# Reordering the attention slots that carry a cycle of the twist network

## The chip, the cores and the metric

The kernel runs as one program on one core of a Trainium2 chip. Its time is the device time in microseconds (us). The core's engines run side by side, each through its own list of instructions in order: TensorE (PE in the profile, PEld for its weight loads), VectorE (DVE), ScalarE (ACT), GpSimd (POOL) and SyncE (SP), which here only issues DMAs. An instruction waits on semaphores that other engines raise, and everything behind it on its own engine waits with it. TensorE writes its results to PSUM, which has eight banks of 128x512 float32.

## The reference, cut to what matters

The model has two layers over `x` of shape (32, 128, 128). The change touches the first layer alone, where an attention is followed by a mixing network:

```python
x = x + attn0(cond(x))             # 16 heads of 64, causal, softmax, output projection
h = recurrence(x)                  # sigmoid gates, two running products, a running sum
gf = global_net(h.mean(axis=1))    # once for each sequence
for _ in range(3):                 # the three cycles of the twist network
    tf = sigmoid(gelu(gelu(gelu(out @ w1) @ w2) @ w3) @ w4)   # 128 -> 128 -> 64 -> 32 -> 1
    coupling = 0.1 + range * (0.7 * gf + 0.3 * tf - 0.5) * 2
    out = out + coupling * twist(out)      # twist: a signed permutation of the 128 features
x = x + out
```

The second layer (routed experts, an attention with small heads, a low-rank layer, slots) follows. It is not touched.

## The kernel before, in words

Everything is float32, with features on the 128 partitions. The 4096 tokens stand as eight chunks of 512 columns, and a chunk is four sequences of 128.

**The slots of the first attention.** The loop `for h in range(NH)` goes over 16 half-chunks (a chunk, and half of its heads), and inside it `for b in range(CB)` goes over four sequences. One pass of the inner loop is called a slot here and is named by h and b: h10 b2. There are 64 of them. A slot pushes one unit of attention, `unit(h, b)` (L462), into a hand-made pipeline, `Staggered(0, 3, 4, 5)` (L825). So a slot does the `scores` of its own unit, then `turned` of the unit three slots older, `values` of the unit four slots older, and, in every fourth slot, `projected` of the unit five slots older.

- `scores` (L474): on TensorE two causal-mask matmuls in bf16 (`causal`, `twice`) that open two PSUM banks, and 32 records of small `qk` matmuls. On VectorE, for each bank, the row maximum (`s_max<-ps`), a tiny minimum (`s_max<-s_max`) and the biased copy `s_sb<-ps,s_max`. On ScalarE four exponentials out of the two banks and one in place. On GpSimd `s_half` and `s_part`, which halve the rows for the sums. On VectorE `s_sum` and its reciprocal. On GpSimd the normalising `s_sb<-s_sb,s_sum`.
- `turned` (L519): six transposes (`ps<-w_base,s_sb`), copied out by ScalarE (`pT`, 512 columns) and VectorE (`pT`, 256 columns).
- `values` (L531): 32 small matmuls (`ps<-pT,v` and `ps<-pT,vo`), copied out by VectorE (`oT`).
- `projected` (L544): four matmuls of 128x512.

Beside the units, a slot takes one step of every running generator (`recurrence`, L556, and `routed`, L680) and three of the twelve `projections` of the next half-chunk: one matmul of 128x512 each, copied out by ScalarE as `qk` or `v`.

**The slots with a cycle.** In seven slots (h6, h7, h8, h10, h11, h12 and h14, always at b2) a cycle of `twisted` (L594) runs for two chunks at once, in steps. A cycle is numbered 0, 1 or 2: h6, h10 and h14 have cycle 0; h7 and h11 cycle 1; h8 and h12 cycle 2.

- `first`: two matmuls of 128x512 (`ps<-F,w_mix`) and two gelus (`h`). `second`, `third`: two smaller matmuls and one gelu each. Cycle 0 adds three tiny matmuls of the global network with activations `g`, `g` and `tg`.
- `fourth` (L648): two matmuls, two tanh (`th<-ps,hb`), and then the coupling. For each chunk: VectorE `th<-th,ar,cB`; GpSimd `v<-th,F` (not in cycle 2); VectorE `th<-th,TF`; VectorE or GpSimd `F<-F,th`; VectorE or GpSimd `tw<-TF,v`; in cycle 2 GpSimd `X<-X,F`. `TF` is the twisted F. In cycle 0 it comes from a matmul with `twist` and stays in a PSUM bank until `tw` has been read out of it; in the other cycles it is in SBUF.

The slot alternates these steps with its three projections: first, projection, second, projection, third, projection, fourth. At h14 `prepared` (L755), some thirty small matmuls for the second layer, runs in the same slot.

**What sets the order.** A scheduler orders each engine's instructions, with two exceptions. Every activation that goes through `act` (L381) keeps the program's order on ScalarE. VectorE and TensorE instructions that are issued while the list `pinned` is not empty keep the program's order among themselves. PSUM banks are handed out by `ps()` (L297) in a ring of eight, `RING = "AABBBCCC"`: a ninth request waits until a bank of the same letter has been read out. Nearly all instructions are recorded at two helper lines, L259 (TensorE, VectorE, GpSimd) and L383 (ScalarE), so they are told apart by their tiles.

Of the kernel before, what the change touches and what calls it, by code (L numbers as in the profile page):

```python
# [11 lines left out]
F32 = mybir.dt.float32  # L12
# [7 lines left out]
P = 128  # L20
# [5 lines left out]
CH = CB * S  # L26
# [192 lines left out]
class Staggered:  # L219
# [7 lines left out]
        self.items.append(stages)  # L227
        self._step()

    def _step(self):  # L230
        for k, lag in enumerate(self.lags):
            n = self.t - lag
            if 0 <= n < len(self.items) and k < len(self.items[n]) and self.items[n][k]:
                self.items[n][k]()
        self.t += 1

    def flush(self):
# [7 lines left out]
def program(ctx, tc, out, xT, packs, where):  # L245
    nc = tc.nc
    pinned = []
# [35 lines left out]
    def w(name):  # L283
        pack, rows, c0, n = where[name]
        return loaded[pack][:rows, c0 : c0 + n]
# [8 lines left out]
    def bank(tag):  # L294
        return psum.tile([P, 512], F32, tag="ps" + tag, name="ps", bufs=RING.count(tag))

    def ps():  # L297
        if short:
            return bank("C")
        turn["all"] += 1  # L300
        return bank(RING[(turn["all"] - 1) % 8])
# [5 lines left out]
    def mm(out_, lhsT, rhs, start=True, stop=True):  # L307
        T.matmul(out_, lhsT=lhsT, rhs=rhs, start=start, stop=stop)

    def inner(ap, n):  # L310

        return ap.unsqueeze(2).to_broadcast([ap.shape[0], ap.shape[1], n])
# [5 lines left out]
    def tt(eng, out_, a, b, op):  # L318
        eng.tensor_tensor(out_, a, b, op)
# [7 lines left out]
    def col(g):  # L327
        return X[:, bass.ts(g, CH)]

    def b3(ap):  # L330

        return ap.rearrange("p (b s) -> p b s", s=S)
# [48 lines left out]
    def act(*args, **kwargs):  # L381

        return tc.keep_in_program_order(A.activation(*args, **kwargs))  # L383
# [7 lines left out]
    tpool = ctx.enter_context(tc.tile_pool(name="t2", bufs=2, side="right"))  # L391
# [34 lines left out]
    def modulated(g):  # L426
        bs = slice(g * CB, (g + 1) * CB)
        xs = qpool.tile([P, CH], F32, tag="xs", name="xs", bufs=1)
        tt(G, b3(xs), b3(col(g)), inner(ysT[:, bs], S), ALU.mult)
        p = ps()  # L430
        mm(p, w("cond_w"), xs)
        hTs[g] = qpool.tile([P, CH], F32, tag="hT", name="hT")
        tt(V, b3(hTs[g]), b3(p), inner(dT[:, bs], S), ALU.mult)
# [120 lines left out]
    Fs = {}  # L554
# [39 lines left out]
    def twisted(g0, cyc, turned):  # L594

        gs = (g0, g0 + 1)
        bs = slice(g0 * CB, (g0 + 2) * CB)
        nb = 2 * CB
        at = {}

        def first():
            at["h1"] = []
            for g in gs:
                p = ps()
                mm(p, w("cn_w1"), Fs[g])
                h1 = mpool.tile([P, CH], F32, tag="h1", name="h1")
                act(h1, p, AF.Gelu, bias=w("cn_b1"))
                at["h1"].append(h1)
            if cyc == 0:
                gct = mpool.tile([P, nb], F32, tag="gct", name="gct")  # L610
                for k, g in enumerate(gs):
                    V.tensor_reduce(gct[:, k * CB : (k + 1) * CB], b3(Fs[g]), AX.X, ALU.add)
                V.tensor_scalar(gct, gct, 1.0 / S, None, ALU.mult)
                p = ps()
                mm(p[:64, :nb], w("gc_w1"), gct)
                at["g1"] = mpool.tile([64, nb], F32, tag="g1", name="g1")
                act(at["g1"], p[:64, :nb], AF.Gelu, bias=w("gc_b1"))

        def second():

            p = ps()
            for k in range(2):
                mm(p[64 * k : 64 * k + 64], w("cn_w2"), at["h1"][k])
            at["h2"] = mpool.tile([P, CH], F32, tag="h2", name="h2", bufs=1)
            act(at["h2"], p, AF.Gelu, bias=w("cn_b2"))
            if cyc == 0:
                p = ps()
                mm(p[:32, :nb], w("gc_w2"), at["g1"])
                at["g2"] = mpool.tile([32, nb], F32, tag="g2", name="g2")
                act(at["g2"], p[:32, :nb], AF.Gelu, bias=w("gc_b2"))  # L630

        def third():
            p = ps()
            for k in range(2):
                r = slice(64 * k, 64 * k + 64)
                mm(p[32 * k : 32 * k + 32], w("cn_w3")[r], at["h2"][r])
            at["h3"] = mpool.tile([64, CH], F32, tag="h3", name="h3", bufs=1)
            act(at["h3"], p[:64], AF.Gelu, bias=w("cn_b3"))
            if cyc == 0:

                p = ps()
                mm(p[:, :nb], w("gc_w3"), at["g2"])
                tg = mpool.tile([P, nb], F32, tag="tg", name="tg")
                act(tg, p[:, :nb], AF.Tanh, bias=hb3, scale=0.5)
                cBs[g0] = mpool.tile([P, nb], F32, tag="cB", name="cB")
                V.tensor_scalar(cBs[g0], tg, ar7, 0.1, ALU.mult, ALU.add)

        def fourth():  # L648
            two = [ps(), ps()]
            for k in range(2):  # L650
                r = slice(32 * k, 32 * k + 32)
                mm(two[k], w("cn_w4")[r], at["h3"][r])
            for k, g in enumerate(gs):
                th = mpool.tile([P, CH], F32, tag="th", name="th")
                act(th, two[k], AF.Tanh, bias=hb4, scale=0.5)
                cB = cBs[g0][:, k * CB : (k + 1) * CB]
                V.scalar_tensor_tensor(b3(th), b3(th), ar3, inner(cB, S), ALU.mult, ALU.add)

                F, TF = Fs[g], turned[k]
                if cyc == 0:  # L660
                    p = ps()
                    mm(p, w("twist"), F)
                    TF = p
                if cyc < 2:
                    v = mpool.tile([P, CH], F32, tag="h1", name="v")
                    tt(G, v, th, F, ALU.mult)
                tt(V, th, th, TF, ALU.mult)
                tt(G if k else V, F, F, th, ALU.add)
                if cyc < 2:
                    tt(V if cyc == 0 else G, turned[k], TF, v, ALU.subtract)  # L670
                if cyc == 2:
                    tt(G, col(g), col(g), Fs[g], ALU.add)

        return [first, second, third, fourth]


    picks = {}
# [143 lines left out]
    NH = 2 * NCH  # L821
# [3 lines left out]
    pipe = Staggered(0, 3, 4, 5)  # L825
    turned = {}
    running = []
    for h in range(NH):


        pieces = projections(h + 1) if h + 1 < NH else []
        for b in range(CB):
            pipe.push(*unit(h, b))
            for gen in list(running):
                if next(gen, gen) is gen:
                    running.remove(gen)
            if b == 1 and h >= 3 and h % 2 == 1:
                gen = recurrence((h - 3) // 2, [apool.tile([P, CH], F32, tag="rec%d" % i, name="rec", bufs=1) for i in range(3)])
                next(gen)
                running.append(gen)  # L840
            if b == 0 and h % 2 == 0 and h + 2 < NH:
                modulated(h // 2 + 1)
            work = []
            k = h - 6
            if h == NH - 1 and b == 2:
                pinned_g.append(True)
            if b == 2 and 0 <= k < NH - 7 and k % 4 < 3:
                if k % 4 == 0:
                    turned = [tpool.tile([P, CH], F32, tag="t2", name="tw") for _ in range(2)]
                work = twisted(2 * (k // 4), k % 4, turned)  # L850
                if h == NH - 2:
                    prepared()
            if b == 3 and k >= 0 and k % 4 == 2:
                running.append(routed(2 * (k // 4)))
            for i in range(4):
                if work:
                    work[i]()
                if i < 3 and pieces:
                    pieces[3 * b + i]()

# [523 lines left out]
    def first_pieces():  # L1386
# [16 lines left out]
        def cycle(g0, cyc, turned, k, n):  # L1403

            several(*ins[k : k + n])
            for i, f in enumerate(twisted(g0, cyc, turned)):
                several(f, *outs[k + i : min(k + i + 1, k + n)])
# [117 lines left out]
    for i in range(END + 2 * TURN):  # L1525
        r, k = i // TURN, i % TURN
# [6 lines left out]
        if r < NP and k == 0:  # L1533
            ins, outs, _ = (p + q for p, q in zip(experts(2 * r), experts(2 * r + 1)))
# [3 lines left out]
        if k >= 24 and r < NP:  # L1538
            b = k - 23
# [49 lines left out]
```

## Time and profile before

| | us |
|---|---|
| median of 3 runs | 1243.85 |
| lowest to highest | 1240.15 to 1244.99 |
| the profiled execution, its own time | 1245.78 |
| its span on the core | 1244.0 |
| TensorE busy | 1093.5 (88%) |
| VectorE busy | 753.7 (61%) |
| ScalarE busy | 694.8 (56%) |
| GpSimd busy | 446.6 (36%) |
| slots of the first attention, first scores to last | 35.6 to 581.5 |

The profile is one execution. Some 2 us lie around its span, and it stands 1.9 us above the median. A group's row gives its busy time, the mean duration in ns of one instruction, and the idle time of the engine ahead of the group with what ended most of it. A row of the timeline gives start, length, engine, operation, tiles and count, and in brackets the idle time of the engine ahead of it and who ended it. A float32 matmul of 128x512 stands in the trace as two records. The granted clock of TensorE is a share of its full speed.

### The profile page before, as it was taken

The numbers are of one execution on the slowest core, as the hardware profiler recorded it, in microseconds if no ns is written. First come the engines' busy times: TensorE is split into PE (matmuls) and PEld (weight loads), VectorE is DVE, ScalarE is ACT, GpSimd is POOL, SyncE is SP. The second block draws the span as 40 slices with busy tenths as digits, with TensorE's granted clock in tenths as the row PEclk, the third lists the DMA queues.
The fourth block names the chain that finished last, engine by engine and source line by source line (L and its number), as shares of the span: only waits on it lengthen the run. The fifth ranks groups of instructions, "written<-read, shape, count | busy, mean of one in ns | idle before, by whom it ended". The sixth has DMA issues, their size and how long they took to land. (4 is left out here: it accounts for less than half of the span.)

```text
span 1244.0 us, 28751 instructions
## 1 busy us (share of the span) xinstructions
PE 1093.5 (88%) x11429; PEld 693.2 (56%) x11429; DVE 753.7 (61%) x2254; ACT 694.8 (56%) x1668; POOL 446.6 (36%) x557
## 2 busy tenths in 40 slices
PE   3999999988999889998888677998999999998774
PEld 1465555445454454554545445776676676676543
DVE  1454858475595755937446478456746674757654
ACT  1655464554646646445455556665875586558631
POOL 1445545435454454523354531133212321222000
PEclk9999999899999999989998898999999999999867
DMA  6000000000000000000242210234023502320000
GB/s 268 18 10 11 9 10 11 9 4 8 9 10 10 3 8 9 10 3 8 97 134 66 85 40 3 70 113 135 11 78 95 162 12 62 110 67 11 2 17 17
DMA packets 23460, 56.46 MB, mean 45 GB/s; under 512 B 2592, under 2 KB 12960, under 8 KB 23072
## 3 DMA queue, kind: packets, MB, share of 16 engines
q0 software_dynamic: 9648, 40.01, 10.3%
q1 hardware_dynamic: 13104, 13.58, 3.7%
q8 instruction: 90, 1.47, 0.5%
q10 hardware_dynamic: 576, 1.05, 0.3%
q14 instruction: 42, 0.34, 0.1%
HBM read 46.25 MB, written 2.10 MB: 39 GB/s over the span
## 5 line engine op out<-in xcount | busy, mean ns | idle before, releaser
L383 ACT ACTIVATE s_sb<-ps,s_max 128x128 f32<-128x128 f32 x256 | 73.8, 366 | 125.3 <-DVE s_sb L259 120.1
L259 PE MATMUL ps<-hT,w_attn 128*128 128x512 f32 x256 | 127.0, 624 | 15.5 <-DVE hT L259 10.1
L259 POOL TENSOR_TENSOR s_sb<-s_sb,s_sum 128x512 f32<-128x512 f32 (+1 forms) x126 | 106.8, 868 | 66.6 <-DVE s_sum L259 59.6
L383 ACT ACT_TABLE_LOAD x63 | 80.8, 1283 | 80.3 <-DVE s_sb L259 66.6
L259 POOL DMA_INDIRECT ew<-in_expert,rows x64 | 63.4, 991 | 130.3 <-DVE ye L259 79.3
L383 ACT ACTIVATE qk<-ps 128x512 f32<-128x512 f32 x128 | 72.5, 607 | 60.6 <-PE ps L259 59.8
L259 DVE TENSOR_REDUCE s_max<-ps 128x6 f32<-128x384 f32 x128 | 64.4, 541 | 50.9 <-PE ps L259 50.8
L259 POOL TENSOR_TENSOR s_half<-s_sb 128x256 f32<-128x256 f32 x62 | 45.8, 739 | 134.1 <-ACT s_sb L383 134.1
L383 ACT ACTIVATE he<-ps,ew 128x128 f32<-128x128 f32 x256 | 71.7, 384 | 32.1 <-issue 18.7
L259 PEld LDWEIGHTS ps<-hT,w_attn 128*128 128x128 f32 x256 | 47.4, 196 | 74.2 <-issue 44.0
L259 PE MATMUL ps<-pT,v 128*64 128x64 f32 (+1 forms) x1536 | 83.8, 229 | 3.5 <-DVE X L259 1.9
L383 ACT ACTIVATE s<-ps,s1max 128x128 f32<-128x128 f32 x256 | 73.1, 390 | 18.9 <-DVE s1max L259 18.9
L259 PEld LDWEIGHTS ps<-pT,v 128*64 128x64 f32 (+1 forms) x1536 | 70.6, 138 | 21.8 <-issue 5.0
L259 PE MATMUL ps<-he,ew 128*128 128x128 f32 x512 | 77.0, 291 | 5.9 <-ACT he L383 4.9
L259 PEld LDWEIGHTS ps<-he,ew 128*128 128x128 f32 x512 | 67.8, 197 | 25.2 <-ACT he L383 12.9
L259 PE MATMUL ps<-X,ew 128*128 128x128 f32 x512 | 76.8, 282 | 0.9 <-DMA ew<-in_expert,rows 0.9
L259 PEld LDWEIGHTS <-twice 128*128 128x128 bf16 x384 | 36.1, 98 | 71.9 <-issue 61.4
L259 DVE TENSOR_REDUCE s1m<-ps 128x6 f32<-128x384 f32 x128 | 65.0, 548 | 16.3 <-PE ps L259 16.3
L259 DVE TENSOR_REDUCE s_sum<-s_part 128x8 f32<-128x256 f32 x62 | 25.8, 415 | 80.6 <-POOL s_part L259 80.5
L259 PEld LDWEIGHTS ps<-X,ew 128*128 128x128 f32 x512 | 67.0, 193 | 11.2 <-issue 9.0
L259 PEld LDWEIGHTS ps<-qk 64*64 64x64 f32 x2048 | 52.7, 136 | 31.6 <-issue 31.6
L259 PE MATMUL ps<-w_base,s 128*128 128x128 f32 x384 | 62.0, 287 | 7.9 <-ACT s L383 4.8
(303 smaller groups left out, 2576.4 us busy)
## 6 DMA issues: line engine op xcount, KB each, us to landing
vo<-v SPq DMA_DIRECT2D x64, 64.0 KB, 1.9
v1o<-v SPq DMA_DIRECT2D x8, 256.0 KB, 3.4
out_x<-ot SPq DMA_DIRECT2D x8, 256.0 KB, 2.3
X<-in_xT ACTq DMA_DIRECT2D x4, 256.0 KB, 7.1
X<-in_xT SPq DMA_DIRECT2D x4, 256.0 KB, 9.9
w_attn<-in_attn POOLq DMA_DIRECT2D x1, 1024.0 KB
w_lowr<-in_lowr SPq DMA_DIRECT2D x1, 1024.0 KB
ew<-in_expert,rows POOLq DMA_INDIRECT x64, 5.0
```

The lines of the kernel that those rows point to most:

```text
L259: ins = f(*args, **kwargs)
L383: return tc.keep_in_program_order(A.activation(*args, **kwargs))
```

## The change

`fourth` is split. What is left of it makes the two matmuls and the tanh, and, in cycle 0, now issues both `twist` matmuls right there, one after the other; the rest becomes a fifth step, `coupled`. The pipeline's push is split too: `older` runs the stages of the older units (`turned`, `values`, `projected`) without the new unit's `scores`, and `newest` runs those scores alone.

A slot with a cycle then goes: `first` of the cycle; the older units' stages; the generators' steps; (at h14 `prepared`); projection, `second`, projection, `third`, projection, `fourth`; the slot's own `scores`; the coupling. Scores and coupling are issued under `pinned`, so VectorE has the scores' maxima ahead of the coupling. Before, it went: `scores`, older units' stages, generators, (`prepared`), `first`, projection, `second`, projection, `third`, projection, `fourth` with the coupling. The 57 other slots have the same steps in the same order. The five cycles that run after the 64 slots, in `first_pieces` (L1386), go through the five steps in turn beside expert pieces; there one expert piece of the first of them now stands ahead of the coupling instead of behind it. The numbers of instructions on TensorE, VectorE and GpSimd stay as they are.

```diff
@@ -227,11 +227,24 @@
         self.items.append(stages)
         self._step()
 
-    def _step(self):
-        for k, lag in enumerate(self.lags):
-            n = self.t - lag
+    def older(self, *stages):
+
+        self.items.append(stages)
+        self._stages(range(1, len(self.lags)))
+
+    def newest(self):
+
+        self._stages(range(1))
+        self.t += 1
+
+    def _stages(self, ks):
+        for k in ks:
+            n = self.t - self.lags[k]
             if 0 <= n < len(self.items) and k < len(self.items[n]) and self.items[n][k]:
                 self.items[n][k]()
+
+    def _step(self):
+        self._stages(range(len(self.lags)))
         self.t += 1
 
     def flush(self):
@@ -650,17 +663,24 @@
             for k in range(2):
                 r = slice(32 * k, 32 * k + 32)
                 mm(two[k], w("cn_w4")[r], at["h3"][r])
+            at["th"] = []
             for k, g in enumerate(gs):
                 th = mpool.tile([P, CH], F32, tag="th", name="th")
                 act(th, two[k], AF.Tanh, bias=hb4, scale=0.5)
+                at["th"].append(th)
+            at["TF"] = turned
+            if cyc == 0:
+                at["TF"] = [ps(), ps()]
+                for k, g in enumerate(gs):
+                    mm(at["TF"][k], w("twist"), Fs[g])
+
+        def coupled():
+            for k, g in enumerate(gs):
+                th = at["th"][k]
                 cB = cBs[g0][:, k * CB : (k + 1) * CB]
                 V.scalar_tensor_tensor(b3(th), b3(th), ar3, inner(cB, S), ALU.mult, ALU.add)
 
-                F, TF = Fs[g], turned[k]
-                if cyc == 0:
-                    p = ps()
-                    mm(p, w("twist"), F)
-                    TF = p
+                F, TF = Fs[g], at["TF"][k]
                 if cyc < 2:
                     v = mpool.tile([P, CH], F32, tag="h1", name="v")
                     tt(G, v, th, F, ALU.mult)
@@ -671,7 +691,7 @@
                 if cyc == 2:
                     tt(G, col(g), col(g), Fs[g], ALU.add)
 
-        return [first, second, third, fourth]
+        return [first, second, third, fourth, coupled]
 
 
     picks = {}
@@ -830,7 +850,15 @@
 
         pieces = projections(h + 1) if h + 1 < NH else []
         for b in range(CB):
-            pipe.push(*unit(h, b))
+            k = h - 6
+            cycle = b == 2 and 0 <= k < NH - 7 and k % 4 < 3
+            work = []
+            if cycle:
+                if k % 4 == 0:
+                    turned = [tpool.tile([P, CH], F32, tag="t2", name="tw") for _ in range(2)]
+                work = twisted(2 * (k // 4), k % 4, turned)
+                work[0]()
+            (pipe.older if cycle else pipe.push)(*unit(h, b))
             for gen in list(running):
                 if next(gen, gen) is gen:
                     running.remove(gen)
@@ -840,23 +868,23 @@
                 running.append(gen)
             if b == 0 and h % 2 == 0 and h + 2 < NH:
                 modulated(h // 2 + 1)
-            work = []
-            k = h - 6
             if h == NH - 1 and b == 2:
                 pinned_g.append(True)
-            if b == 2 and 0 <= k < NH - 7 and k % 4 < 3:
-                if k % 4 == 0:
-                    turned = [tpool.tile([P, CH], F32, tag="t2", name="tw") for _ in range(2)]
-                work = twisted(2 * (k // 4), k % 4, turned)
-                if h == NH - 2:
-                    prepared()
+            if cycle and h == NH - 2:
+                prepared()
             if b == 3 and k >= 0 and k % 4 == 2:
                 running.append(routed(2 * (k // 4)))
-            for i in range(4):
+            for i in range(3):
+                if pieces:
+                    pieces[3 * b + i]()
                 if work:
-                    work[i]()
-                if i < 3 and pieces:
-                    pieces[3 * b + i]()
+                    work[i + 1]()
+            if work:
+
+                pinned.append(True)
+                pipe.newest()
+                work[4]()
+                pinned.pop()
 
 
 
```

## The prediction

> **What bounds the kernel now.** I read the page first, for what is busy and what the clock does.
>
> ```profile
> span 1244.0 us, 28751 instructions
> ...
> PE 1093.5 (88%) x11429; PEld 693.2 (56%) x11429; DVE 753.7 (61%) x2254; ACT 694.8 (56%) x1668; POOL 446.6 (36%) x557
> ...
> PEclk9999999899999999989998898999999999999867
> ```
>
> TensorE leads with 88%. Averages hide the stage, so next come the windows view, for one plain slot (h2 b2) and for the three slots b2, b3, b0 around a cycle: cycle 0 (h10), cycle 1 (h11), cycle 2 (h12). The columns are length, then busy time by engine, then the granted clock.
>
> ```profile
> core 0: us, PE busy (x) PEld busy (x) DVE busy (x) ACT busy (x) POOL busy (x), PEclk, DMA share, GB/s
> 95.00:100.95 5.95, 5.95 (x79) 3.74 (x78) 3.20 (x11) 3.61 (x9) 3.16 (x5) 1.00 0.01 3
> 375.52:407.82 32.30, 30.21 (x269) 15.37 (x268) 15.85 (x41) 18.08 (x40) 15.55 (x21) 1.00 0.04 9
> 416.36:455.81 39.45, 31.82 (x262) 16.21 (x260) 28.86 (x52) 18.70 (x37) 20.55 (x23) 0.91 0.03 8
> 461.76:491.33 29.57, 27.86 (x259) 14.22 (x258) 16.99 (x46) 17.22 (x35) 14.96 (x20) 1.00 0.04 10
> ```
>
> A plain slot is all TensorE. Around a cycle 1 TensorE stands still for 7.6 of 39.45 us, and part of the rest runs at half clock. The timeline of that stretch says who it waits for (start, length, idle before):
>
> ```profile
> 421.46 1.02 PE L259 MATMUL ps<-hT,w_attn 128*128 128x512 f32 x2
> 426.24 1.22 PE L259 MATMUL ps<-h,w_mix 128*64 128x512 f32 x3 [3.76 <-ACT h L383]
> ...
> 443.57 0.32 PE L259 MATMUL ps<-causal,twice 128*128 128x384 bf16 x1 [3.88 <-ACT s_sb L383]
> ...
> 424.20 1.28 ACT L383 ACT_TABLE_LOAD   x1
> 425.50 1.26 ACT L383 ACTIVATE h<-ps,w_base 128x512 f32<-128x512 f32 x2
> ...
> 441.60 1.28 ACT L383 ACT_TABLE_LOAD   x1 [6.68 <-DVE s_sb L259]
> ...
> 436.99 1.77 DVE L259 TENSOR_TENSOR th<-th,tw 128x512 f32<-128x512 f32 x1 [1.19 <-POOL v L259]
> 438.68 0.54 DVE L259 TENSOR_REDUCE s_max<-ps 128x6 f32<-128x384 f32 x1
> ```
>
> Two stalls. First: `first` ended at 421.5, but its gelus started at 425.5, because ScalarE had this slot's exponentials and two table loads ahead of them, and those waited for VectorE. Second: h11 b3's scores were ready at 434.8, but VectorE reached their `s_max` only at 438.7, behind the coupling that waited for GpSimd's `v`; ScalarE stood 6.68 us, the ring of banks ran full, and h12 b0's scores waited until 443.57. The change goes at both.
>
> **Prices on TensorE, from the timeline at full clock:** scores 1.25 us (416.36 to 417.61), transposes 0.80 (to 418.41), values 1.23 (to 419.64), one 128x512 matmul 0.86 (415.50 to 416.36). In the cycle 2 of h12, `second` 1.0, `third` 1.0 (471.16 to 472.14), `fourth` 1.06 (473.19 to 474.25). Other prices: table load 1.28; two gelus or tanh 1.26; `pT` 0.61; `s_max` 0.54; from the end of scores to ScalarE's release of the first bank 3.0 (1.0 of VectorE, 1.28 of table load, 0.6 of exponentials), of the second 3.6.
>
> **Nothing is removed but two table loads**, and no DMA moves: SP's list is the same, and GpSimd issues none in these slots. Where a recurrence's sigmoids come just ahead (h7, h11), the exponentials no longer stand between sigmoid and gelu: 2 x 1.28 us. ScalarE's page in the Trainium skill ("ScalarE: Activation LUTs", "What ACT_TABLE_LOAD costs") counts a drain beside the load, 2.66 us in all, and by it this would be 5.3 instead of 2.6. The trace decides for 1.28: an ACTIVATE starts 0.02 us after the load ends, and no gap stands ahead of it.
>
> **Cycle 1 (from 416.36).** `first` 1.8, transposes and values to 3.8: ScalarE finishes the projections' `qk` at 0.9, loads to 2.1, makes both gelus by 3.4, `pT` by 4.0. So `second` finds its input ready. Then projection 0.9, `second` 1.0, projection, `third`, projection, `fourth`, scores: the slot's scores end at 11.0, and h11 b2 as a slot ended at 17.2 before. The gelus between the steps (0.69) lie under the projections (0.86); bare, each would add 0.69.
> The next bound is VectorE. By the built program's order the recurrence's work comes ahead of the slot's `s_max`: reciprocals to 2.9, a wait for GpSimd's two products (2.62) until 5.6, eight scans (2.85, from 595.98 to 598.85), GpSimd's product 1.26, scan 1.22, two operations of 0.69, ending at 12.3; where GpSimd holds VectorE up as it did for the 1.77 above (0.69 alone), at 14. So `s_max` comes 1.3 to 3 late. TensorE goes on with h11 b3's scores, transposes, values and one projection (4.1) to 15.1, then waits for the first bank until 15.3 to 17. Two projections, scores, transposes, values, `projected`, `xs` and a projection are 10.2: 25.5 to 27.2. The next bank hangs on h12 b0's exponentials, whose `s_max` is queued on VectorE behind a coupling that waits for GpSimd (normalising 1.61, then `v` 1.3 twice): free at 28 to 30. Two more projections: 29.8 to 31.7. A half-clock stretch adds up to 1.7 (below). I take 32.4 against 39.45: **7.0 gained at h11, 6.5 at h7** (38.81 before); bounds 5.4 to 9.6.
>
> **Cycle 2 (from 461.76).** Same chain without a recurrence: scores end at 11.0, h12 b3 ends at 16.8, h13 b0 at 26.2, against 29.57. No bank is late by the rows: those of h12 b3's second and third projection are free at 14.1 and 14.7, where TensorE comes at 15.1 and 16.0. The coupling, now later, still ends before the next reader of F. **3.3 gained, twice**; bounds 2 to 3.4.
>
> **Cycle 0: here the change adds a wait.** The two `twist` matmuls (1.72) now stand ahead of the slot's scores, so two banks are held until the coupling's `tw` has read them, and the coupling comes after two units' maxima. Slot scores end at 13.1 (the cycle 1 sum, plus 1.72 and 0.4 of small matmuls). From there: first exponentials 3.5, `s_half` and `s_part` to 5.1, `s_sum` and reciprocal to 5.8, GpSimd's normalising to 7.45, the next unit's `s_half` to 8.2, `v` to 9.4, VectorE's `th`, `s_sum`, `F`, `tw` to 12.1. The second chunk's `tw` follows at 15.5. So the banks come free 25.2 and 28.6 into the stretch.
> By the built order, at h10 the first of them is that of h10 b3's `values`, and queued behind it on TensorE are a projection (the other bank), h11 b0's values, `projected` and three projections. TensorE comes at 20.0, waits 5.2, and 2.2 more: the stretch ends at 36.9 against 32.30. With half clock for one or two windows of 3.41 us (1.7 each) it is 38.6 to 40.3; I take 38.3, **6.0 lost**. At h6 the ring stands differently: the first late bank is that of h7 b0's values, a wait of 3.0, and the end is 33.1 to 34.8 against 35.82 (which held 6.8 us of half clock): **1.0 gained**. At h14 the matmuls of `prepared` now cover the gelus of `first`, and h15 has no projections behind the held banks: **1.0 gained**. Bounds: h10 8 to 4.6 lost, h6 1 lost to 2.7 gained, h14 1 lost to 1.8 gained.
>
> **The clock.** Half clock came in windows of multiples of 3.41 us, and not only after long stops: at 239.86 after a stop of 1.03 us, and at 427.59 and 444.66 after the two stalls above. The skill ("TensorE: Matmul & The Clock Gate", Part 1) asks for an idle window of about 3.4 us; by that rule only h10's 5.2 us wait would halve the clock, and cycle 1 would gain 1 more. The trace decides, so each new stop of over 1 us may cost up to 1.7.
>
> **Sum.** 6.5 + 7.0 + 3.3 + 3.3 + 1.0 + 1.0 - 6.0 = 16.1 off the profiled execution's 1245.78: 1229.7. That execution stands 1.9 above the median, so 1243.85 - 16 = **1228 us**. Later stages have the same work and take the shift over. Best bounds together: 25.9 less; worst: 4.8 less.
>
> **Rivals.** *A: VectorE takes over.* Around a cycle 1 it has 28.86 us of busy time, and the trace's 1.77 for 0.69 shows GpSimd stretching it. If each move only shifts the queue, cycle 1 gains 4 and cycle 2 gains 1.5, so 2 x 4 + 2 x 1.5 + 2 - 6 = 7 less: 1237. For it: VectorE's 28.86 against the 32.4 I leave it. Against: some of that is stretched by waiting.
> *B: slower. The held `twist` banks decide.* Place: h6, h10, h14, TensorE behind `values` and projections, until GpSimd has normalised and made `v`. Price: 5.2 + 2.2 of waits and two half-clock windows, near 10 us in each of three slots, 30, against 20.1 from cycles 1 and 2 and 2 less of friction: some 12 slower, 1256. It decides once a cycle 0 loses over 6.7 us in the mean. Against: at h6 and h14 the banks fall to later users.
> *C: the waits are covered.* No window of half clock follows and GpSimd's chain is 2 us shorter: h10 loses 2 instead of 6, h6 and h14 gain 2 more each, cycle 1 gains 3 more each. That is 4 + 4 + 6 more: 1214.
>
> **Numbers.** A difference of 0.5% (6.2 us) is about what a measurement can tell from none: faster means below 1237.6. Forecast 0.62 (own range 1220 to 1236), A 0.18, B 0.10, C 0.10. A lies on the border, half to each side: faster 0.62 + 0.10 + 0.09 = 0.81, same 0.09, slower 0.10. Range 1218 to 1241: from the best bounds through A; B and most of C are left out.
>
> **What would show it.** Right: in h7 and h11 no stop of TensorE ahead of `second`, `s_max` of the slot and of the next ahead of `th`, ScalarE's 6.68 us wait gone, 61 table loads for 63, b2 to the next b1 near 32 us. At h10 a stop of TensorE of some 5 us ahead of `ps<-pT,v`, ended by VectorE's `tw`, and near 38 us for the stretch. Wrong: stops ahead of `ps<-pT,v` in all three cycle 0 slots with half clock behind them (B), or cycle 1 still above 35 us with `s_max` late (A).

## The result, and the profile after

The changed kernel takes 1252.08 us (median of 16 runs, 1246.14 to 1255.0) against 1243.99 for the kernel before on the same chip: ratio 1.0053, 95% interval 1.0041 to 1.0066. It is 0.5% slower, where 1228 was forecast. The profiled execution has 1249.83 us, 4.1 above that of the kernel before, where the medians are 8.1 apart, so the traces account for about half of the loss. Its page (first the span, then busy time by engine, then the granted clock by fortieths of the span):

```profile
span 1247.9 us, 28751 instructions
...
PE 1096.3 (88%) x11429; PEld 693.7 (56%) x11429; DVE 756.1 (61%) x2254; ACT 692.3 (55%) x1666; POOL 450.0 (36%) x557
...
PEclk9999999899998989998989898999999999999875
...
L396 ACT ACT_TABLE_LOAD x61 | 78.3, 1283 | 49.1 <-DVE s_sb L272 33.8
```

ScalarE has two table loads fewer (the last row is that group, with its busy time, the ns of one and the idle time ahead of it); otherwise nothing on the page says where the time went. The windows view does. Since a slot with a cycle now has its scores at its end, I cut from the scores of one b1 to those of the next. In order: h7 (cycle 1), h8 (cycle 2), h9 (no cycle), h10 (cycle 0), h11 (cycle 1).

```profile
core 0: us, PE busy (x) PEld busy (x) DVE busy (x) ACT busy (x) POOL busy (x), PEclk, DMA share, GB/s
251.94:293.45 41.51, 36.98 (x346) 18.97 (x345) 30.34 (x60) 22.98 (x47) 22.47 (x25) 0.99 0.03 8
293.45:327.06 33.61, 33.61 (x338) 18.27 (x336) 19.96 (x47) 19.10 (x42) 18.13 (x23) 0.96 0.04 9
327.06:365.39 38.33, 33.84 (x337) 19.21 (x336) 33.68 (x92) 19.98 (x47) 19.16 (x27) 0.96 0.03 9
365.39:411.50 46.11, 38.45 (x350) 20.77 (x349) 21.34 (x56) 21.34 (x48) 19.57 (x27) 0.89 0.03 7
411.50:454.23 42.73, 38.20 (x346) 19.49 (x344) 30.78 (x61) 23.63 (x48) 23.14 (x26) 0.94 0.03 7
```

The same stretches in every kernel of this study, read from the trace in the same way, in us. A stretch is named by the half-chunk that it starts in, and h14 runs on to the scores of h15 b2. "Rest" is from the last scores of the first attention to the end of the span; "ratio" is against the kernel before on the same chip, with its 95% interval.

| kernel | h6 | h7 | h8 | h9 | h10 | h11 | h12 | h13 | h14 | rest | ratio |
|---|---|---|---|---|---|---|---|---|---|---|---|
| cycle | 0 | 1 | 2 | none | 0 | 1 | 2 | none | 0 | | |
| before | 41.9 | 47.3 | 35.4 | 34.3 | 38.7 | 48.0 | 35.5 | 33.5 | 53.4 | 662.5 | |
| after | 42.8 | 41.5 | 33.6 | 38.3 | 46.1 | 42.7 | 33.8 | 37.2 | 53.6 | 665.9 | 1.0053 (1.0041 to 1.0066) |
| e1_add_first | 41.3 | 42.7 | 32.6 | 38.1 | 47.2 | 42.7 | 32.8 | 37.0 | 52.8 | 669.1 | 1.0028 (1.0012 to 1.0044) |
| e2_cycle1_only | 38.9 | 42.8 | 36.3 | 34.3 | 38.7 | 42.6 | 35.6 | 33.5 | 56.4 | 663.1 | 0.9929 (0.9908 to 0.9950) |
| e3_cycle0_only | 42.6 | 47.4 | 35.4 | 34.3 | 45.9 | 48.8 | 35.5 | 33.5 | 52.8 | 665.8 | 1.0091 (1.0070 to 1.0112) |
| e4_cycle2_only | 38.9 | 48.1 | 32.6 | 39.0 | 38.7 | 49.4 | 32.8 | 37.5 | 53.5 | 664.8 | 1.0005 (0.9990 to 1.0021) |
| e5_twist_late | 38.6 | 43.0 | 33.3 | 38.4 | 38.9 | 43.0 | 33.5 | 37.3 | 49.1 | 664.0 | 0.9890 (0.9871 to 0.9909) |
| e6_older_first_at_h9 | 41.3 | 42.4 | 32.8 | 37.6 | 52.2 | 42.7 | 33.6 | 35.5 | 59.3 | 665.9 | 1.0047 (1.0026 to 1.0069) |
| e7_c12_older_first | 38.9 | 42.8 | 33.4 | 36.2 | 43.8 | 42.5 | 32.5 | 34.4 | 61.7 | 667.1 | 1.0021 (1.0010 to 1.0033) |
| e8_c1_chunk1_later | 38.9 | 38.3 | 40.6 | 34.8 | 38.7 | 38.4 | 39.6 | 34.0 | 53.5 | 667.0 | 0.9940 (0.9919 to 0.9961) |
| e9_gate_later | 38.6 | 43.0 | 33.6 | 37.3 | 41.8 | 42.6 | 33.2 | 37.5 | 53.5 | 665.8 | 0.9962 (0.9948 to 0.9976) |
| e10_v_on_vector | 38.6 | 39.2 | 34.0 | 38.7 | 38.9 | 40.1 | 33.3 | 38.0 | 52.3 | 658.6 | 0.9856 (0.9833 to 0.9878) |
| e11_all | 38.6 | 39.2 | 34.0 | 37.3 | 43.5 | 40.2 | 33.3 | 36.2 | 53.2 | 663.6 | 0.9893 (0.9872 to 0.9914) |
| e12_old_cycle2 | 38.6 | 39.2 | 37.1 | 34.3 | 38.9 | 41.0 | 37.5 | 33.5 | 50.7 | 664.2 | 0.9818 (0.9789 to 0.9847) |

From before to after, cycles 1 gain 5.8 + 5.3, cycles 2 gain 1.8 + 1.8, cycles 0 lose 0.9 + 7.4 + 0.1, and h9 and h13, which hold no cycle, lose 4.0 + 3.8. The sum is 1.5 lost, and the rest of the kernel 3.4 more. From the first scores to those of h6 b1, ahead of any cycle, every kernel took 174.5 or 174.6. The kernels ran on several chips, so whole times are compared by their ratios here, and stretches by the traces, of which there is one for each kernel.

**Cycle 1 at h11**, in the timeline (start, length, engine, operation, tiles and count; in brackets the idle time ahead and who ended it; rows of TensorE, then ScalarE, then VectorE):

```profile
424.77 1.08 PE L272 MATMUL ps<-h,w_mix 128*64 128x512 f32 x4
...
450.65 3.78 PE L272 MATMUL ps<-hT,w_attn 128*128 128x512 f32 x4 [3.84 <-ACT s_sb L396]
...
434.32 1.28 ACT L396 ACT_TABLE_LOAD   x1 [3.03 <-DVE s_sb L272]
...
449.97 0.63 ACT L396 ACTIVATE s_sb<-ps,s_max 128x128 f32<-128x128 f32 x2 [9.62 <-DVE s_sb L272]
...
443.27 1.51 DVE L272 TENSOR_TENSOR th<-th,tw 128x512 f32<-128x512 f32 x1 [2.15 <-POOL v L272]
...
448.91 0.69 DVE L272 TENSOR_TENSOR th<-th,tw 128x512 f32<-128x512 f32 x1 [0.51 <-POOL v L272]
449.52 0.15 DVE L272 TENSOR_TENSOR s_max<-s_max 128x2 f32<-128x2 f32 x1
```

The stop of 3.76 us ahead of `second` is gone (`ps<-h,w_mix` has no bracket; `first` began at 420.03), and the one of 3.88 us behind the coupling has moved by one unit: it is now 3.84 us ahead of a projection in h12 b0. The scores of that b0 were done at 439.4, but VectorE stands on the coupling's `th<-th,tw` for GpSimd's `v`, and the minimum that the biased copy and the exponentials need comes at 449.5. The two projections behind the stop take 3.78 us where at full clock four records took 1.98.

**Cycle 0 at h10**, the held banks, and **h9**, which nobody had on the list:

```profile
398.05 1.42 PE L272 MATMUL ps<-pT,v 128*64 128x64 f32 x17 [5.35 <-DVE tw L272]
...
401.47 2.08 PE L272 MATMUL ps<-w_attn,hT 128*128 128x512 f32 x2 [1.25 <-DVE tw L272]
...
395.55 0.69 DVE L272 TENSOR_TENSOR th<-th,ps 128x512 f32<-128x512 f32 x1 [3.40 <-POOL v L272]
...
332.05 0.88 PE L272 MATMUL ps<-pT,v 128*64 128x64 f32 x17 [2.78 <-DVE X L272]
...
327.71 0.91 DVE L272 TENSOR_REDUCE r_seg<-X 128x8 f32<-128x336 f32 x2 [0.57 <-POOL X L272]
...
331.33 0.67 DVE L272 TENSOR_TENSOR X<-X,ps 128x512 f32<-128x512 f32 x1
...
326.40 1.27 POOL L272 TENSOR_TENSOR X<-X,F 128x512 f32<-128x512 f32 x1
```

At h10 the first wait is the forecast one, 5.35 for 5.2; the second is 1.25 for 2.2. At h9 b1 `values` waits for a bank that `projected` had filled by 324.6: the add that reads it out, `X<-X,ps`, stands on VectorE behind the sums `r_seg` of `routed`, which stand behind the last `X<-X,F` of cycle 2's coupling on GpSimd. The same stop (2.62 us) is in h13 b1.

### The profile page after: what moved, and what is told of

Its sections match the earlier page's. It is cut to its first block, busy times and chain, and to the rows that moved or that the text cites. A ratio compares the mean times of both kernels' runs of the same rounds, so it can differ in the third digit from the quotient of the medians.

```text
span 1247.9 us, 28751 instructions
## 1 busy us (share of the span) xinstructions
PE 1096.3 (88%) x11429; PEld 693.7 (56%) x11429; DVE 756.1 (61%) x2254; ACT 692.3 (55%) x1666; POOL 450.0 (36%) x557
## 5 line engine op out<-in xcount | busy, mean ns | idle before, releaser
L272 PE MATMUL ps<-hT,w_attn 128*128 128x512 f32 x256 | 130.0, 635 | 23.1 <-ACT s_sb L396 13.0
L272 POOL TENSOR_TENSOR s_sb<-s_sb,s_sum 128x512 f32<-128x512 f32 (+1 forms) x126 | 110.2, 896 | 55.7 <-DVE s_sum L272 49.2
L396 ACT ACT_TABLE_LOAD x61 | 78.3, 1283 | 49.1 <-DVE s_sb L272 33.8
L272 PEld LDWEIGHTS <-twice 128*128 128x128 bf16 x384 | 35.7, 100 | 61.7 <-issue 50.6
L272 PE MATMUL ps<-w_attn,hT 128*128 128x512 f32 x128 | 64.6, 622 | 5.8 <-DVE s_sb L272 4.4
## 6 DMA issues: line engine op xcount, KB each, us to landing
w_lowr<-in_lowr SPq DMA_DIRECT2D x1, 1024.0 KB, 12.7
```

The lines of the kernel that those rows point to most:

```text
L272: ins = f(*args, **kwargs)
```

## The experiments

Theory at the start: three places make the loss, the held twist banks (h6, h10, h14), the later `X<-X,F` of cycle 2 (h9, h13), and a rest of cycle 1 behind GpSimd's `v`. Rival: the places are one chain, in which a gain at one slot is paid back at the next whatever its order, or the loss lies in the clock and in the stages after the first attention.

### One cycle at a time: e2, e3, e4

The new order is taken for one cycle number alone. The slots of the others, and the cycles after the 64 slots, go as in the kernel before (in e3 with the twist matmuls as in the changed kernel).

```diff
+            fresh = cycle and k % 4 in (1,)     # (0,) in e3, (2,) in e4
-            (pipe.older if cycle else pipe.push)(*unit(h, b))
+            (pipe.older if fresh else pipe.push)(*unit(h, b))
...
+            if cycle and not fresh:
+                work[0]()                       # old order: scores first, first to coupling behind
```

Cycle 1 alone: 

> New order in the slots of cycle 1 alone (h7 b2, h11 b2); the slots of cycles 0 and 2 and the cycles after the 64 slots as in the kernel before. Theory (each slot's gain is its own and is kept): the stretches of h7 and h11 are 5.8 and 5.3 us shorter as in the changed kernel's trace, nothing else moves, 11 us below the kernel before: 1233. Rival (TensorE's wait comes back in the next slots, since VectorE and the ring of banks run later): h8 and h12 lose 3 or more each, 1238 to 1241.

Cycle 0 alone: 

> New order in the slots of cycle 0 alone (h6, h10, h14, at b2); the others as in the kernel before. Theory (held twist banks): h10 loses 7.4 us as in the changed kernel's trace, h6 0.9 and h14 0.1: 8 above the kernel before, 1252. Rival (h10's loss needed the late start that the changed cycles 1 and 2 of h7 and h8 left behind): 0 to 3 above, 1244 to 1247.

Cycle 2 alone: 

> New order in the slots of cycle 2 alone (h8, h12, at b2); the others as in the kernel before. Theory: the stretches of h8 and h12 gain 1.8 to 3.3 each, and the later X<-X,F stops VectorE ahead of the add that frees projected's bank, so h9 b1 and h13 b1 lose 3.8 to 4.0 each: 1 to 4 above the kernel before, 1245 to 1248. Rival (the stop of h9 and h13 comes from what cycles 0 and 1 left behind): 4 to 6 below, 1238 to 1240.

Measured 0.9929, 1.0091 and 1.0005. On the scale of the 1244 us before, these are 1235, 1255 and 1245, each nearer to its theory than to the rival. Together they come to 0.25% slower, where the changed kernel has 0.53%, which the intervals allow. In each run the stretches of its own cycle are within 1.3 us of the changed kernel's, so the effects are local for the most part. **Cycle 1** gains 4.6 and 5.4 and gives back 0.9 in h8. (At h6 and h14 the order of e2 is the old one; h6 is 3.0 shorter there and h14 3.0 longer, with 6.8 us of half clock less and 6.8 more.) **Cycle 0** alone loses 7.2 in h10, with the same stops of 5.35 and 1.25 us ended by `tw`; it needs nothing of cycles 1 and 2. **Cycle 2** alone is the cause of h9 and h13:

```profile
295.84:328.41 32.57, 32.57 (x338) 17.56 (x336) 17.86 (x43) 18.77 (x40) 14.85 (x18) 1.00 0.04 9
328.41:367.44 39.03, 34.88 (x337) 20.14 (x336) 33.11 (x92) 20.06 (x47) 19.12 (x27) 0.91 0.04 9
```

```profile
333.37 1.42 PE L272 MATMUL ps<-pT,v 128*64 128x64 f32 x17 [2.77 <-DVE X L272]
```

The first fence is its windows, the second its timeline. Its own stretch (first row, h8) has TensorE busy from end to end and is 2.8 shorter than before, close to the forecast 3.3. The next one (h9) has the same stop as in the changed kernel, with half clock behind it, and loses 4.7. Cycle 2 by itself is a wash.

### The twist matmuls behind the scores: e5

```diff
             at["TF"] = turned
-            if cyc == 0:
-                at["TF"] = [ps(), ps()]
-                for k, g in enumerate(gs):
-                    mm(at["TF"][k], w("twist"), Fs[g])
...
                 F, TF = Fs[g], at["TF"][k]
+                if cyc == 0:
+                    TF = ps()
+                    mm(TF, w("twist"), F)
```

> The changed kernel, but the twist matmuls of cycle 0 stand in the coupling, behind the slot's scores, each chunk's just ahead of its products. Theory 1 (the banks are taken too early): the wait of TensorE ahead of h10 b3's values falls away, h10's stretch goes from 46.1 back to 39 to 41, the whole to 1244 to 1247. Theory 2 (what counts is how late the coupling's tw reads the bank, and the coupling stays behind the maxima of two units): the wait only moves to another user of the ring, h10 keeps more than 5 of its 7.4, and the whole stays at 1249 to 1253.

Measured: 0.9890 of before, where the changed kernel has 1.0053; more than theory 1 asked for. In the windows view (h6, h10, h14):

```profile
209.67:248.27 38.60, 36.67 (x347) 19.50 (x346) 20.82 (x51) 21.43 (x48) 18.06 (x25) 1.00 0.03 8
363.03:401.97 38.94, 37.18 (x350) 19.80 (x349) 21.09 (x54) 21.45 (x48) 18.05 (x25) 1.00 0.03 8
515.84:564.91 49.07, 46.21 (x471) 28.14 (x470) 26.74 (x73) 22.78 (x54) 19.45 (x28) 1.00 0.03 6
```

Against the changed kernel that is 4.2 + 7.2 + 4.5 = 15.9 us. At h10 two stops of 5.35 and 1.25 us have become this:

```profile
388.20 1.13 PE L272 MATMUL ps<-w_attn,hT 128*128 128x512 f32 x2 [0.53 <-ACT s_sb L396]
...
393.56 0.32 PE L272 MATMUL ps<-causal,twice 128*128 128x384 bf16 x1 [0.65 <-DVE tw L272]
```

The coupling's `tw` still reads the banks late: the first read starts 12.7 us behind the start of the slot's own scores, 13.0 in the changed kernel. But asked for behind the scores, they are another two places of the ring, and the next users of those come later: h11 b0's scores wait 0.65 us where h10 b3's `values` waited 5.35. No stop of these stretches reaches 0.7 us, and the clock column is 1.00 in all three rows. Theory 2 falls.

### Taking the wait out of h9: e1, e6, e7, e9

e1 keeps the add ahead of the sums on VectorE:

```diff
+            if h in (7, 11):
+                pinned.append(True)
             tt(V, col(g), col(g), p, ALU.add)
+            pinned.clear()
...
+            pinned.append(True)
             V.tensor_reduce(seg[:, k, :], x3[:, :, s0:s1], AX.X, ALU.add)
+            pinned.pop()
```

> The changed kernel, but on VectorE the add X<-X,ps of the half-chunks h7 and h11 is kept ahead of the r_seg sums that wait for GpSimd's X<-X,F. Theory (the queue on VectorE): h9 b1 and h13 b1 lose their stop of 2.6 to 2.8 us ahead of values and the half clock behind it; the stretches h9 b1 to h10 b1 and h13 b1 to h14 b1 go from 38.3 and 37.2 back to 34.3 and 33.5, and the whole is 7 to 8 us below the changed kernel, near 1244. Rival 1 (something else holds a bank at the same place, for instance h8 b3's exponentials): the stop stays or moves, less than 2 us. Rival 2 (the extra time lies after the first attention): the two stretches fall, the time from the last scores to the end grows by as much, 1250 to 1252.

Measured 1.0028, h9 at 38.1 and h13 at 37.0: a miss for the theory as it stood, and rival 1. The wait was split rather than removed:

```profile
329.54 0.88 PE L272 MATMUL ps<-pT,v 128*64 128x64 f32 x17 [1.22 <-DVE X L272]
331.49 0.29 PE L272 MATMUL ps<-w_moe,r_agg 128*8 128x4 f32 x6 [0.65 <-DVE r_agg L272]
...
345.04 0.32 PE L272 MATMUL ps<-causal,twice 128*128 128x384 bf16 x1 [1.90 <-ACT s_sb L396]
...
328.28 0.42 DVE L272 TENSOR_REDUCE s_sum<-s_part 128x8 f32<-128x256 f32 x1 [2.08 <-POOL s_part L272]
...
328.85 0.64 DVE L272 TENSOR_TENSOR X<-X,ps 128x512 f32<-128x512 f32 x1
```

Now the add stands behind `s_sum`, which waits for the exponentials of h9 b0, whose maxima stand behind the coupling; and TensorE's own gate matmul of `routed` waits for `r_agg`. The third stop, 1.90 us ahead of h9 b3's scores, does not stand in the changed kernel. Half clock is gone from h9 (3.4 us before the repair), and the stretch is as long as it was.

e6 adds to e1 that in h9 b0 and h13 b0 the older units' parts go first and the slot's scores last; e7 is that with cycle 0 in the old order:

```diff
+            first_older = b == 0 and h in (9, 13)
-            (pipe.older if cycle else pipe.push)(*unit(h, b))
+            (pipe.older if cycle or first_older else pipe.push)(*unit(h, b))
+            if first_older:
+                pinned.append(True)
+                pipe.newest()
+                pinned.pop()
```

> As the earlier kernel with the adds ahead of the r_seg sums, and in h9 b0 and h13 b0 the older units' parts (projected among them) go ahead of the slot's scores, so that VectorE has the add X<-X,ps ahead of that slot's s_max. Theory (VectorE's queue in order: the add stood behind s_sum, which waits for the scores' exponentials, whose s_max stands behind the coupling): no stop of TensorE ahead of h9 b1's and h13 b1's values, the two stretches fall from 38.3 and 37.2 to 34 to 35.5, 6 to 8 less than the changed kernel: 1243 to 1246. Rival (late s_max of that slot holds its own two banks, and the stop comes some matmuls later): the stretches stay above 36.5, at most 3 less: 1248 to 1251.

> New order for cycles 1 and 2, old order for cycle 0, with the repair of h9 b0 and h13 b0 as in the kernel sent with it. Theory: the gains add, cycle 1 9.9 and cycle 2 5.6 as they showed alone, and of cycle 2's 8.8 of loss in h9 and h13 at most 2 are left: 1229 to 1234. Rival (the stop only moves): cycle 2 gives nothing, and the time is that of cycle 1 alone, 1235 to 1238.

Measured 1.0047 and 1.0021, or 1250 and 1247 on the scale of 1244: e6 is where its rival has it, e7 some 8 us above its own. `values` of h9 b1 has no stop any more (the add now runs at 324.5), but the gate matmul of `routed`, next on TensorE, has all of it, and the scores moved in b0 cost more behind it. At h10 (52.2 and 43.8) a new stop of 2.3 us stands ahead of transposes, ended by the next `X<-X,ps`; at h14 (59.3 and 61.7) `values` waits 2.85 us for that add, 0.33 in the changed kernel; and more half clock follows both. The gate matmul in e6:

```profile
333.34 0.29 PE L272 MATMUL ps<-w_moe,r_agg 128*8 128x4 f32 x6 [2.92 <-DVE r_agg L272]
```

e9 goes back to e5 and starts `routed` one slot later, with the add pinned ahead of the sums as in e1, so that neither stands behind GpSimd in h9 b1:

```diff
-            if b == 3 and k >= 0 and k % 4 == 2:
-                running.append(routed(2 * (k // 4)))
+            if b == 0 and k >= 1 and k % 4 == 3:
+                running.append(routed(2 * ((k - 1) // 4)))
```

> The changed kernel with the twist matmuls behind the scores (the late twist kernel), and routed is started one slot later (first step in h9 b1, h13 b1) with its r_seg sums behind the add X<-X,ps. So neither VectorE's add nor TensorE's gate matmul ps<-w_moe,r_agg, which waits for r_agg, stands behind GpSimd's X<-X,F in h9 b1. Theory (two waits one behind the other, the add and the gate matmul): the stops of 2.8 and 2.6 us in h9 b1 and h13 b1 go, with the half clock behind them; the two stretches go from 38.4 and 37.3 to 34.3 and 33.5, and the whole is 6 to 8 below the late twist kernel: 1226 to 1228 where that has 1234. Rival (the late s_max of h9 b0 is the last bound anyway): less than 3 us gained, 1231 to 1234.

Measured 0.9962, worse than e5's 0.9890 and than the rival. In h9 a stop of 1.22 us ahead of `values` is left, a new one of 2.38 us follows ahead of a transpose, and h10 loses 2.9, where VectorE has the later steps of `routed` ahead of the add of the next `projected`. What these four show together: in h9 the coupling, `routed` and a recurrence share VectorE within three slots (33.7 us of busy time in a stretch of 38.3; before, 29.7 in 34.3), and an order that frees one waiter stops the next. A repair of h9 was not found.

### The rest of cycle 1: e8, e10

e8 takes e2 and issues the coupling's second chunk behind the scores of the next b0:

```diff
-        def coupled():
-            for k, g in enumerate(gs):
+        def coupled(ks=(0, 1)):
+            for k in ks:
+                g = gs[k]
...
+            if late and b == 0:
+                pinned.append(True)
+                pipe.items.append(unit(h, b))
+                pipe._stages(range(1))
+                pinned.pop()
+                pipe._stages(range(1, 4))
+                pipe.t += 1
+                pinned.append(True)
+                late.pop()((1,))
+                pinned.pop()
...
-                work[4]()
+                work[4]((0,) if k % 4 in (1,) else (0, 1))
+                if k % 4 in (1,):
+                    late.append(work[4])
```

> New order for cycle 1 alone, and the coupling of its second chunk is issued behind the scores of the next b0 (h8, h12), pinned. Theory (what is left of cycle 1's stops is the 3.8 us in h8 b0 and h12 b0, where s_max waits on VectorE behind the second chunk's th, which waits for GpSimd's v): that stop and its half clock go, the stretches of h7 and h11 fall from 42.8 and 42.6 to 37 to 39, the whole is 7 to 12 below cycle 1 alone: 1225 to 1230. Rival (VectorE and GpSimd are simply late there, and the second chunk stops a later unit as long): the stretches or the ones after lose it again, 1234 to 1239.

Measured 0.9940, no better than e2's 0.9929. h7 and h11 fall by 4.5 and 4.2 as the theory has it, and h8 and h12 give back 4.3 and 4.0: VectorE still waits for `v`, now ahead of b1's maxima. The 3.8 us stop becomes five of 0.3 to 1.2 us and one of 1.8 us. The rival was right.

e10 removes the wait instead of moving it, on top of e5:

```diff
-                    tt(G, v, th, F, ALU.mult)
+                    tt(V if cyc in (1,) else G, v, th, F, ALU.mult)
```

> The late twist kernel, with cycle 1's product v on VectorE (two more 128x512 products there, about 0.7 us each) in place of GpSimd. Theory (in cycle 1 VectorE's th<-th,tw stands waiting for GpSimd's v, which is queued behind the normalising, and the s_max of h8 b0 stands behind it): TensorE's 3.8 us stop in h8 b0 and h12 b0 shrinks to under 1.5, h7 and h11 go from 43.0 to 37 to 40, 6 to 12 below the late twist kernel: 1222 to 1228. Rival (VectorE is the bound there, 28.9 us busy before, and gets 1.4 more): h7 and h11 stay at 42 to 44, 1233 to 1236.

Measured 0.9856 (0.9833 to 0.9878) against e5's 0.9890 (0.9871 to 0.9909): 4 us less, with intervals that overlap a little. In the traces the two stretches are 6.8 us shorter, near what the theory has. VectorE has two products more and is done sooner (windows of h7 and h11, then the timeline of h11):

```profile
247.61:286.76 39.15, 36.61 (x345) 19.00 (x344) 32.33 (x64) 21.88 (x45) 21.38 (x23) 1.00 0.03 8
398.34:438.48 40.14, 36.73 (x346) 18.92 (x345) 32.35 (x64) 22.85 (x48) 22.36 (x25) 1.00 0.03 8
```

```profile
435.31 1.12 PE L272 MATMUL ps<-hT,w_attn 128*128 128x512 f32 x2 [1.38 <-ACT s_sb L396]
437.51 1.13 PE L272 MATMUL ps<-hT,w_attn 128*128 128x512 f32 x2 [1.08 <-ACT s_sb L396]
...
427.91 1.18 DVE L272 TENSOR_TENSOR v<-th,F 128x512 f32<-128x512 f32 x1
```

The stop of 3.8 us is now two of 1.38 and 1.08, the rows have no half clock, and VectorE is busy for 32.3 of 39.2 and 40.1 us: the rival's bound may be what is left, which no run tests. The edit also takes two products from GpSimd's list; whether the wait for `v` or that shorter list made the gain is not told apart.

### Together: e11 and e12

e11 has both edits, e9's and e10's. 

> Both edits of the two kernels sent with it on top of the late twist kernel. If both theories hold and the gains are local: 13 to 18 below the late twist kernel, 1216 to 1221. If only the first: 1226 to 1228; if only the second: 1222 to 1228; if neither: 1231 to 1236.

Measured 0.9893, no better than e5's 0.9890: the loss of e9 at h10 (43.5) stands, and cycle 1's gain of e10 with it, each in its place.

e12 is e10 with cycle 2 in the old order in its slots (the edit of e2 with `k % 4 in (0, 1)`). 

> The kernel with the late twist and cycle 1's v on VectorE, with the slots of cycle 2 (h8, h12) in the order of the kernel before. Theory (cycle 2's new order loses in h9 and h13 more than it gains in h8 and h12, as it did alone): h9 and h13 go from 38.7 and 38.0 back to 34.3 and 33.5, h8 and h12 from 34.0 and 33.3 to 35.5 to 37: 3 to 6 below, ratio to the kernel before 0.981 to 0.983, near 1221. Rival (behind a cycle 1 that ends late, cycle 2 in the old order loses the same again in its own slot, h8 and h12 at 38 or more): no gain, 0.985 to 0.987.

Measured 0.9818 (0.9789 to 0.9847) against e10's 0.9856 (0.9833 to 0.9878). h9 and h13 return to 34.3 and 33.5 as the theory has it, and h8 and h12 pay 3.1 and 4.2, more than it allowed: in the trace the two pairs gain 1.3 and 0.3. The intervals overlap, so whether cycle 2 is better old or new behind a good cycle 1 stays open. Both kernels beat the kernel before and the changed one: 1.8% and 1.4% under the former.

## Why the prediction was wrong

Its own sum, term by term (forecast, then measured, in us of gain): cycle 1 13.5 and 11.1; cycle 2 6.6 and 3.6; cycle 0 -4.0 and -8.4; h9 and h13 0 and -7.8. Together 16.1 and -1.5: of the 17.6 that are missing, 7.8 were no term at all. (By the medians 24 are missing. The rest behind the first attention has 3.4 of that, and most of what is left is how far the two profiled executions lie from their medians.)

**The step that failed most** is the sentence on cycle 2, "The coupling, now later, still ends before the next reader of F." It looked for readers of F alone. The coupling of cycle 2 also writes X, and X has readers on VectorE that queue ahead of work that frees banks. e4 shows it alone: 2.8 + 2.7 gained in the slots, 4.7 + 4.1 lost behind them. The readers of X are one part of it: in e1, where they no longer stand ahead of the add, the next unit's maxima, which stand behind the same coupling, still delay it.

**Cycle 0: the waits were right, their place in the account was wrong.** Forecast at h10 was a wait of 5.2 and one of 2.2; they are 5.35 and 1.25. At h6 a wait of 3.0 was forecast and is 2.63. But half clock followed in all three slots (10.2 us at h10, 6.8 at h6 and at h14), and at h14 the 2.63 us wait ahead of `values` was no term. The base had its share of luck: the kernel before had 6.8 us of half clock at h6 and h14 too, and at h6 the same instructions in e2 had none and took 38.9 for 41.9. Held banks cost 15.9 us in the three slots, measured by e5, where the sum had 6.0 in one. Rival B had the mechanism; its price (near 10 each) was too high, and its verdict came true by luck, with the 7.8 of h9 and h13 that it did not know of. The prediction took the early matmuls as given and did not ask what the same order would give without them: e5, at 0.9890 of the kernel before, is 14 us under it, near the 16 that the change was forecast to bring.

**Cycle 1: the chain was right, its last link short.** `first` to the end of the slot's scores takes 11.2 (11.0 forecast), `s_max` comes 2.1 late (1.3 to 3), the wait for the first bank is 0.69. The next bank was put at 28 to 30 us after `first` and comes free at 30.6, and the half clock behind it lasts 6.8 us. So the stretch from `first` to the next b1 is 34.2 for 32.4 at h11. The bound named for it, VectorE behind GpSimd's `v`, is the one that e10 loosens by 3.9 and 2.9. Rival A's number for the two cycles 1 (4 each) is nearer at h11 than the forecast's 7; its reason was VectorE's load, and e10, which adds to that load and is faster in these stretches, speaks against it.

**Cycle 2: right in its own slot.** 2.8 and 2.7 alone for 3.3; in the changed kernel 1.8 each, because half clock left by cycle 1's stop reaches into the stretch (the clock column of h8 is 0.96 there and 1.00 in e4).

**Table loads: right.** 61 for 63, at 1283 ns each.

**"Later stages have the same work and take the shift over" is left open by one profile each.** The rest took 3.4 us more in the changed kernel's profile. But from TensorE's last 5,900 instructions to the end (the last 950, 1,300 and 170 of ScalarE, VectorE and GpSimd also stand in the same order) before, after, e1 and e5 take 604.6, 609.9, 610.1 and 605.7 us, with 75.7, 88.5, 91.9 and 79.1 us of half clock. e5, with the same order, is 4.2 us shorter there than the changed kernel. So the half clock of one execution makes as much difference as the 3.4, and how much of it belongs to the change is not shown.

**The range** (1218 to 1241) lay below the kernel before throughout, with 0.10 for slower. Its worst bounds together, 4.8 less, held no term for an effect outside the slots with a cycle.

## What to carry to other kernels

When a block of work is moved back, list every tile that it writes and every reader of each, then ask on each reader's engine what is queued behind it and which buffer that work frees. A bank taken early from a ring costs by who asks for that place next: here taking it later was enough (15.9 us), though it was read as late as before. Where an engine waits in order for another's product, making the product itself (1.2 us here) can be cheaper than a reordering around the wait, by the traces: over h7 and h8 together e10 gains some 3 us on e5, the reordering e8 0.2 on e2.

## What the runs showed of the hardware

- **Half clock depends on where a stop falls.** The same instructions around h6 with the same two stops (0.51 and 1.03 us before, 0.51 and 1.02 in e2) were followed by 6.8 us of half clock in one profile and by none in the other, 3.0 us of difference; a stop of 2.77 us was followed by 6.8 us in e4, one of 2.78 by 3.4 in the changed kernel, and e10's two of 1.38 and 1.08 by none. In each of the 14 profiles all windows of half clock start on one grid of 3.413 us, to within 0.002 us, and the grid lies elsewhere in each. Cut the time from 60 to 570 us by that grid: in 52 pieces at full clock TensorE was idle for 1.96 us or more, and half clock followed all 52; with 1.5 to 1.95 us it followed 6 of 38; with less, 11 of 1909. Those 11 have hardly a stop, but are filled with the narrow matmuls of `prepared` (`ps<-ah,w_lowr`, 128x32). So a stop of 2 us is dear where it falls into one piece, and may cost no clock where a border of the grid divides it. The Trainium skill ("TensorE: Matmul & The Clock Gate", Part 1) calls the window of about 3.4 us free-running, which the grid agrees with. It also asks for a whole idle window before the clock falls; 1.96 us of idle time in one was always enough here. Windows of half clock between h6 and the last scores sum to 27 us before, 41 after, 20 in e5.
- **VectorE and GpSimd shut each other out.** In the changed kernel a minimum over 128x2 that takes 0.15 us elsewhere took 1.22 us from 323.90, and GpSimd's `X<-X,F` ran until 325.10. That `X<-X,F` took 1.75 us from 323.35 (1.27 elsewhere), while VectorE's `th<-th,tw` ran until 323.99. The skill ("SBUF — State Buffer", "SBUF: two separate sides") has the shared port pair as an exclusive lock between a VectorE operation with two SBUF inputs and a GpSimd operation that reads SBUF: whichever starts first holds it for its whole instruction. The times fit that, and in e10 `v` on VectorE took 1.18 and 1.29 us beside GpSimd, not 0.7.
